# Two gathers in one product, sums evacuated bank by bank: a graph attention layer with gathered neighbours

## The chip, the cores and the metric

The kernel runs on one core of a Trainium2 chip. The metric is the device time of one execution in microseconds. The time before is the median of three runs. A hardware profile comes from one further execution.

## The reference

Two layers work on 4096 nodes of 128 features and a random 4096 x 4096 adjacency of density 1/128, so that a node has some 32 neighbours.

Layer 0 is graph attention with eight heads. For a head with weights `W`, node n weighs its neighbours m:

```
Wh  = nodes @ W                       # per head
e   = leaky_relu(f1[n] + f2[m], 0.2)  # f1 = Wh . a1, f2 = Wh . a2
att = softmax(where(adj > 0, e, -9e15))
h   = elu(att @ Wh)                   # heads side by side: 1024 features
x   = layernorm(nodes + elu(h @ W1 + b1))
```

Layer 1 takes, for each node and feature, three quantiles over the values of its neighbours (some neighbours left out by a rule), mixes their mean with the node's own value, and applies one 128 x 128 matrix.

## The kernel before

**Stages.** A search on DVE and PE turns each adjacency row into a list of at most 64 neighbours. Nodes are then ranked by their count, and 128 nodes of similar count form a tile; `CAPS` gives for each tile the number of neighbour slots it must hold. There are 32 tiles in three blocks of 2, 8 and 22 (`BLOCKS`). While the tiles of block 0 and 1 are weighed, the search for the next block runs between them; the tiles of block 2 have no search beside them. When all are done, layer 1 (`quantile_out`) gathers values again and runs a selection network on DVE.

**Attention of one tile.** The sum over neighbours is taken on the raw node rows, and `W` is applied afterwards. `layers(cap)` cuts the slots into layers of 32, 16, 8 or 4. `fetch_rows` loads the tile's records (SP queue), transposes indices and f1 scores (DVE) and issues one indirect gather per slot column on POOL's queue (line 185), 128 rows each of 137 words: 128 features, a one, eight f2 scores. In a layer of w slots, one gathered column g holds all w slots of k = 128 / w nodes. The rows go into the buffers `G` (32 columns; two of them, and in block 2 a third in another pool) or `Gs` (16 columns, two).

`weigh_rows` then does, per layer: `z` = exp(leaky_relu(f2 + f1)) (DVE lines 829 and 830, ScalarE line 831); `pf`, the weights spread over the columns of the nodes that own them (DVE line 835, 1024 elements a partition); and one product per gathered column (PE line 847), `pf` piece by rows, with 129 columns: weighted features and, from the one, the denominator. Its output goes to `y`, three PSUM banks that hold eight blocks of 129 columns; a block is 16 nodes times 8 heads on 128 partitions. A 32-slot layer gives 32 products into 32 partitions each, a 16-slot layer 16 into 64, a small layer 8 into 128. The products of one layer are finished before those of the next layer.

When all layers are summed, DVE takes the denominators out of PSUM (`rden`, lines 868 and 875) and writes the normalised sums `yn` to SBUF (line 879). PE transposes `yn` in two halves (`turned`, line 896), ScalarE copies them to `yT` (line 897). For two or four tiles together, `transform` applies `W`, elu, `W1`, elu and the layer norm, and the rows go out by scatters on POOL's queue (line 194, `x_d`).

**Order.** `step` fetches tile i and then weighs tile i-1, so POOL gathers one tile ahead. `weigh_rows` is a generator; after each of its yields ("turns") `step` runs one turn of a waiting `transform` and a share of the search pieces:

```
turns = sum(2 + -(-w // 8) for w, *_ in parts) + 3
each = -(-quota // turns)
```

With `quota` 48 pieces a tile in block 0 and 33 in block 1. In these two blocks the order on DVE, PE and ScalarE is as written (`manual_schedule`); in block 2 a scheduler orders the instructions. `pp` holds the PSUM tiles `y` (three banks), `turned`, `o` and `hT`; `key` of the search has the last two banks.

Of the kernel before, what the change touches and what calls it, by code (L numbers as in the profile page):

```python
# [9 lines left out]
F32 = mybir.dt.float32  # L10
# [3 lines left out]
ALU = mybir.AluOpType  # L14
# [6 lines left out]
P = 128  # L21
N = 4096
D = 128
H = 8
# [4 lines left out]
TINY = 1e-30  # L29
# [33 lines left out]
LMAX = 2 * max(HT)  # L63
LMOST = 2 * sorted(HT)[-2]
TURN = 12


R_NUM, R_OWN, R_F1 = L, L + 1, L + 2
# [6 lines left out]
def layers(c):  # L75


    out = []
    s = 0
    for w in (32, 32, 16, 8, 4):  # L80
        if (c + 3) // 4 * 4 - s >= w:
            out.append((s, w))
            s += w
    return out
# [124 lines left out]
def kernel(  # L209
# [135 lines left out]
    def step(fetch=None, pieces=None, quota=0, size=2, more=None):  # L345
        if fetch:
            weigh.append(fetch_rows(tc, pools, narrow[turn[0] % 2], *fetch, xt_d, bad, uses))
            turn[0] += 1
        while store:
            scatter(nc, x1_d, *store.pop(0))  # L350
        if len(weigh) > 1 or (weigh and not fetch):
            R, parts = weigh.pop(0)
            place = len(members)
            members.append(R)
            turns = sum(2 + -(-w // 8) for w, *_ in parts) + 3
            each = -(-quota // turns)
            done = 0
            for _ in weigh_rows(tc, attp, pools, pp, parts, turned, place, size, consts):
                if tails and next(tails[0], True):
                    tails.pop(0)  # L360
                for _ in range(min(each, quota - done)):
                    next(pieces, None)
                    done += 1
            quota -= done
            if len(members) == size:
                tails.append(
                    transform(tc, attp, pp, more or pp, turned.pop(0), list(members), consts, store)
                )
                members.clear()
        elif not fetch:  # L370
            while tails:
                if next(tails[0], True):
                    tails.pop(0)
        for _ in range(quota):
            next(pieces, None)
# [379 lines left out]
def fetch_rows(tc, ap, narrow, rec_d, i, cap, t, xt_d, bad, turn):  # L755

    nc = tc.nc

    R = take(ap, [P, REC], "R", turn, 5)
    rows = rec_d[ts(i, P), :]  # L760
    for u, v in enumerate(rows.rearrange("(g u) w -> u g w", u=4)[k] for k in range(4)):
        nc.sync.dma_start(R[ts(u, 32), :], v)
    for s0, w in layers(cap):
        if w == 32:
            continue
        r = 32 // w
        lists, scores = narrow[w]
        v = rows.rearrange("(g b r) w -> b g r w", b=4, r=r)
        for b in range(4):
            here = slice(32 * b, 32 * b + w)  # L770
            nc.sync.dma_start(
                lists[here, :].rearrange("p (r j) -> p r j", r=r),
                v[b].bitcast(I32)[:, :, s0 : s0 + w],
            )
            nc.sync.dma_start(scores[here], v[b][:, :, R_F1 : R_F1 + H])
    nc.vector.tensor_scalar(
        bad[:, 4, t : t + 1], R[:, R_NUM : R_NUM + 1], float(cap), None, ALU.is_gt
    )
    f1x32 = None
    parts = []  # L780
    G, col = None, 0
    for s0, w in layers(cap):
        k = P // w
        idx = ap[0].tile([P, 32], I32, name="idx", bufs=6)
        if w == 32:
            nc.vector.transpose(idx, R.bitcast(I32)[:, s0 : s0 + w])
            scores, r = R[:, R_F1 : R_F1 + H].unsqueeze(1), 1
        else:
            lists, scores = narrow[w]
            r = 32 // w  # L790
            nc.vector.transpose(idx, lists)
        if w < 32 or f1x32 is None:
            f1b = ap[0].tile([P, H, 32], F32, name="f1b", bufs=1)
            nc.vector.tensor_copy(
                f1b.rearrange("p h (r j) -> p r h j", r=r),
                scores.unsqueeze(3).to_broadcast([P, r, H, 32 // r]),
            )
            f1x = ap[0].tile([P, 32 * H], F32, name="f1x", bufs=6)
            nc.vector.transpose(f1x, f1b.rearrange("p h g -> p (h g)"))
        if w == 32:  # L800
            f1x32 = f1x
        f1v = f1x.rearrange("p (h g) -> p g h", h=H)[:, 0:w, :]
        if w == 32:
            G, col = take(ap, [P, 32, XW], "G", turn), 0
        elif s0 % 32 == 0:

            few = sum(v for s, v in layers(cap) if s >= s0) <= 16
            G, col = take(ap, [P, 16 if few else 32, XW], "Gs" if few else "G", turn), 0
        for g in range(w):
            gather(nc, G[:, col + g, :], xt_d, idx[:, g : g + 1])  # L810
        parts.append((w, k, G[:, col : col + w, :], f1v))
        col += w
    return R, parts


def weigh_rows(tc, ap, pools, pp, parts, turned, place, size, consts):


    nc = tc.nc
    own, ident = consts["own"], consts["ident"]  # L820

    y = pp.tile([P, 3, 512], F32, name="y")

    def block(b):
        return y[:, b // 3, (b % 3) * (D + 1) : (b % 3 + 1) * (D + 1)]

    for i, (w, k, G, f1v) in enumerate(parts):
        z = ap.tile([P, 32, H], F32, name="z")[:, 0:w, :]
        nc.vector.tensor_tensor(z, G[:, :, D + 1 :], f1v, ALU.add)
        nc.vector.scalar_tensor_tensor(z, z, ALPHA, z, ALU.mult, ALU.max)  # L830
        nc.scalar.activation(z, z, AF.Exp)  # L831
        yield
        pf = ap.tile([P, H * P], F32, name="pf")
        spread = [P, w, k, H]
        nc.vector.tensor_tensor(
            pf.rearrange("p (g k h) -> p g k h", g=w, k=k),
            z.unsqueeze(2).to_broadcast(spread),
            own[w].unsqueeze(1).unsqueeze(3).to_broadcast(spread),
            ALU.mult,
        )  # L840
        yield
        last = i == len(parts) - 1
        m = min(k * H, P)
        for g in range(w):
            for c in range(g * k * H, (g + 1) * k * H, m):
                b, p0 = c // P, c % P
                nc.tensor.matmul(  # L847
                    block(b)[p0 : p0 + m, :],
                    lhsT=pf[:, c : c + m],
                    rhs=G[:, g, 0 : D + 1],  # L850
                    start=(i == 0 and b % 3 == 0),
                    stop=last,
                    skip_group_check=True,
                )
            if g % 8 == 7 or g == w - 1:
                yield

    rden = ap.tile([P, H], F32, name="rden")
    yn = ap.tile([P, H, P], F32, name="yn", bufs=1)
    spans = ((0, 2, 6), (2, 1, 2))  # L860
    views = []
    for bank, banks, n in spans:
        c = n // banks
        views.append(
            y[:, bank : bank + banks, 0 : c * (D + 1)].rearrange("p a (c d) -> p a c d", c=c)
        )
    for (bank, banks, n), v in zip(spans, views):
        nc.vector.tensor_scalar(  # L868
            rden[:, 3 * bank : 3 * bank + n].rearrange("p (a c) -> p a c", a=banks),
            v[:, :, :, D],  # L870
            TINY,
            None,
            ALU.max,
        )
    nc.vector.reciprocal(rden, rden)
    for (bank, banks, n), v in zip(spans, views):
        here = slice(3 * bank, 3 * bank + n)
        c = n // banks
        nc.vector.tensor_tensor(
            yn[:, here, :].rearrange("p (a c) d -> p a c d", a=banks),  # L880
            v[:, :, :, 0:D],
            rden[:, here]
            .rearrange("p (a c) -> p a c", a=banks)
            .unsqueeze(3)
            .to_broadcast([P, banks, c, D]),
            ALU.mult,
        )
    yield
    if place == 0:
        wide = [P, H, size * P]  # L890
        turned.append(pools[0 if size == 2 else -1].tile(wide, F32, name="yT" if size == 2 else "yT4", bufs=1))
    yT = turned[-1]
    for half in range(2):
        t_ps = pp.tile([P, 4, P], F32, name="turned")
        for b in range(4):
            nc.tensor.transpose(t_ps[:, b, :], yn[:, 4 * half + b, :], ident)  # L896
        nc.scalar.copy(  # L897
            yT[:, :, ts(place, P)].rearrange("p h (u g) -> p g u h", u=4)[:, ts(half, 16)],
            t_ps.rearrange("p b (g u h) -> p (b g) u h", u=4, h=H),
        )  # L900
        yield
# [493 lines left out]
```

## Time and profile before

| | us |
|---|---|
| runs | 4465.6, 4467.9, 4470.0 (median 4467.9) |
| profiled execution | 4423.5 |
| its span, first to last instruction | 4421.7 |

| engine | busy us | share of the span |
|---|---|---|
| PE matmul | 975.6 | 22% |
| PE weight load | 518.4 | 12% |
| DVE | 2531.5 | 57% |
| ScalarE (ACT) | 1028.7 | 23% |
| POOL | 2301.1 | 52% |

How to read the profile: a group's row names line, engine, operation, output and input tile, the count, the busy time with the mean duration in ns, and the idle time of the engine just before these instructions with what ended it. "issue" as the end of a wait means that nothing in the trace released the engine. A row of waits gives who waited for whom, then the total in us, the number of waits and the longest. A row of the timeline gives start, duration, engine, line, operation, names, count, and in brackets the idle time before it. A row of windows gives a stretch, its length, busy time and number of instructions of PE, PE's weight loads, DVE, ScalarE and POOL, the granted share of PE's clock, the busy share of the DMA engines, and GB/s. An fp32 product of PE stands in the trace as two records, each with a weight load; a transpose as one.

### The profile page before, as it was taken

How to read it: one execution, taken by the hardware profiler on the slowest of the kernel's cores; microseconds unless marked ns; L12 is line 12 of the kernel's file. 1: busy time of each engine (PE TensorE's matmuls, PEld its weight loads, DVE VectorE, ACT ScalarE, POOL GpSimd, SP SyncE). 2: the span in 40 equal slices, each digit the busy share in tenths (PEclk: the TensorE clock that was granted, in tenths of full speed). 3: DMA queues.
4: the chain of work that ended last, by engine and by line, in shares of the span. 5: the costliest groups of instructions: out<-in, count | busy, mean ns of one | idle time of the engine just before them, and what ended most of it. 6: DMA issues, size and time to landing. Idle time of an engine off the chain costs nothing. (4 is left out here: it accounts for less than half of the span.)

```text
span 4421.7 us, 19775 instructions
## 1 busy us (share of the span) xinstructions
PE 975.6 (22%) x4289; PEld 518.4 (12%) x4289; DVE 2531.5 (57%) x4862; ACT 1028.7 (23%) x1424; POOL 2301.1 (52%) x2453
## 2 busy tenths in 40 slices
PE   4323544443223133223243000000000001000101
PEld 2001211111112011121122000000000000000001
DVE  5554556555322114112121437888878999999897
ACT  2101212111000011000010213333333444434343
POOL 2433443344667666757564675666575334455530
PEclk9955555556556555555565555555555555555555
DMA  5313323221121121212111111111111001111100
GB/s 169 108 47 113 99 90 111 86 92 42 48 50 50 47 56 44 57 42 56 44 49 32 48 52 39 48 46 47 35 49 37 23 21 33 31 36 36 38 28 3
DMA packets 115233, 241.26 MB, mean 55 GB/s; under 512 B 51904, under 2 KB 68288, under 8 KB 106912
## 3 DMA queue, kind: packets, MB, share of 16 engines
q0 software_dynamic: 76224, 161.01, 13.2%
q10 hardware_dynamic: 12160, 68.49, 4.4%
q1 hardware_dynamic: 26720, 10.41, 1.1%
q14 instruction: 93, 0.76, 0.1%
q8 instruction: 36, 0.59, 0.1%
HBM read 228.56 MB, written 11.18 MB: 54 GB/s over the span
## 5 line engine op out<-in xcount | busy, mean ns | idle before, releaser
L1145 DVE TENSOR_TENSOR vals<-low,vals 128x1024 f32<-128x1024 f32 (+9 forms) x1359 | 1401.9, 1057 | 332.5 <-ACT low L1141 110.6
L185 POOL DMA_INDIRECT G<-xt_d,idx x1092 | 1066.0, 976 | 729.1 <-issue 399.3
L185 POOL DMA_INDIRECT vals<-x_d,idx x960 | 910.6, 948 | 296.0 <-issue 282.3
L1141 ACT COPY low<-vals 128x1024 f32<-128x1024 f32 (+10 forms) x701 | 607.2, 876 | 969.7 <-DVE vals L1145 658.1
L1155 PE MATMUL st_ps<-ident,u 128*128 128x128 f32 x344 | 86.9, 436 | 1773.9 <-ACT u L1154 1445.8
L577 DVE MAX8 first<-key 128x8 f32<-128x128 f32 x1024 | 223.5, 282 | 342.5 <-remote 207.6
L194 POOL DMA_INDIRECT out_dram<-o,own_i x32 | 31.8, 992 | 619.0 <-ACT o L1167 616.5
L847 PE MATMUL y<-G,pf 128*32 128x129 f32 (+2 forms) x2224 | 211.5, 398 | 525.7 <-issue 428.9
L1155 PEld LDWEIGHTS st_ps<-ident,u 128*128 128x128 f32 x344 | 75.5, 325 | 1785.0 <-ACT u L1154 1453.5
L571 PE MATMUL key<-sgn,markb 128*128 128x512 bf16 x256 | 147.8, 577 | 529.2 <-DVE first L577 358.3
L868 DVE TENSOR_SCALAR rden<-y 128x6 f32<-128x6 f32 x64 | 7.3, 152 | 398.9 <-PE y L847 217.8
L847 PEld LDWEIGHTS y<-G,pf 128*32 128x32 f32 (+2 forms) x2224 | 141.9, 171 | 599.5 <-issue 483.0
L550 ACT ACTIVATE sgn<-adj_t 128x2048 bf16<-128x2048 int32 x64 | 122.0, 1906 | 355.8 <-PE key L571 177.1
L897 ACT COPY yT<-turned 128x512 f32<-128x512 f32 x64 | 65.5, 1024 | 554.8 <-PE turned L896 356.0
L917 DVE TENSOR_SCALAR e<-e 128x512 f32<-128x512 f32 x64 | 28.4, 444 | 241.0 <-issue 203.8
L573 PE MATMUL key<-parts,oneb 64*128 64x512 bf16 x256 | 146.5, 572 | 1.1 <-issue 1.0
L925 PE MATMUL o<-hv,W_sb 128*128 128x256 f32 (+1 forms) x176 | 105.3, 717 | 143.8 <-DVE hv L919 53.5
L194 POOL DMA_INDIRECT x_d<-x,R x32 | 33.4, 1044 | 194.6 <-DVE x L986 161.8
L1145 DVE TENSOR_TENSOR most<-low,most 128x1024 f32<-128x1024 f32 (+7 forms) x116 | 131.8, 1166 | 2.6 <-issue 0.5
L185 POOL DMA_INDIRECT Gs<-xt_d,idx x92 | 89.7, 975 | 77.8 <-PE y L847 46.1
L584 DVE MAX8 rec<-first 128x8 f32<-128x256 f32 x256 | 109.2, 426 | 30.8 <-remote 16.9
L831 ACT ACTIVATE z<-z 128x256 f32<-128x256 f32 (+3 forms) x62 | 20.3, 329 | 452.0 <-DVE z L830 351.6
(187 smaller groups left out, 1795.9 us busy)
## 6 DMA issues: line engine op xcount, KB each, us to landing
adj_t<-in_adj_dram ACTq DMA_DIRECT2D x64, 1024.0 KB
G<-xt_d,idx POOLq DMA_INDIRECT x1092
vals<-x_d,idx POOLq DMA_INDIRECT x960
R<-rec_d SPq DMA_DIRECT2D x128, 26.4 KB
xt_d<-rec SPq DMA_DIRECT2D x4, 548.0 KB
score<-rec_d SPq DMA_DIRECT2D x132, 1.0 KB
rec<-in_x_dram SPq DMA_DIRECT2D x4, 512.0 KB
Gs<-xt_d,idx POOLq DMA_INDIRECT x92
```

Source lines behind the costliest of these rows:

```text
L185: nc.gpsimd.indirect_dma_start(out=dst, out_offset=None, in_=rows, in_offset=bass.IndirectOffsetOnAxis(ap=idx, axis=0),)
L550: nc.scalar.activation(sgn, adj_t, AF.Sign, accum_out=cnt[:, i : i + 1])
L571: nc.tensor.matmul(key, lhsT=markb, rhs=sgn[:, ts(b, 512)], start=True, stop=False)
L573: nc.tensor.matmul(key, lhsT=oneb[0:64, :], rhs=parts[:, c0 : c0 + 512], start=False, stop=True)
L577: nc.vector.max(first[:, ts(c0 // CW + c, 8)], key[:, ts(c, CW)])
L584: nc.vector.max(top, first)
L847: nc.tensor.matmul(block(b)[p0 : p0 + m, :], lhsT=pf[:, c : c + m], rhs=G[:, g, 0 : D + 1], start=(i == 0 and b % 3 == 0), stop=last, skip ...
L897: nc.scalar.copy(yT[:, :, ts(place, P)].rearrange("p h (u g) -> p g u h", u=4)[:, ts(half, 16)], t_ps.rearrange("p b (g u h) -> p (b g) u ...
L925: nc.tensor.matmul(o, lhsT=consts["W1_sb"][:, h, :], rhs=hv[:, ts(j, n)], start=(h == 0), stop=(h == H - 1),)
L1141: nc.scalar.copy(kept, low)
L1145: nc.vector.tensor_tensor(high if end else low, kept, high, ALU.max if end else ALU.min)
L1155: nc.tensor.matmul(st_ps, lhsT=u, rhs=ident, start=(i == 0), stop=(i == len(terms) - 1))
```

## The change

All layers' `z` are computed first. Then the tile is worked through in two halves of four blocks. For each half, `pf` is written for every layer (512 elements a partition). For each block there is one PSUM bank, `y`, out of three in turn. In a 32-slot layer (and in a 16-slot layer where that is the widest), the `pf` pieces of two gathered columns are loaded together, and both columns' rows are streamed side by side: 258 columns. Of the four parts of the product, the two where weights and rows belong to the same gathered column are wanted. The other layers stream their one column twice, so that both halves of the bank receive it. ScalarE then copies the wanted halves, 32 or 64 partitions at a time, to `raw` in SBUF, and DVE normalises `raw` in place.

The turns counted for the search pieces change with the new yields, and `Gs` has 12 columns.

```diff
+YBANKS = 3
...
-            turns = sum(2 + -(-w // 8) for w, *_ in parts) + 3
+            turns = len(parts) + 13
...
-            few = sum(v for s, v in layers(cap) if s >= s0) <= 16
-            G, col = take(ap, [P, 16 if few else 32, XW], "Gs" if few else "G", turn), 0
+            few = sum(v for s, v in layers(cap) if s >= s0) <= 12
+            G, col = take(ap, [P, 12 if few else 32, XW], "Gs" if few else "G", turn), 0
...
-    y = pp.tile([P, 3, 512], F32, name="y")
...
+    zs = []
+    for w, k, G, f1v in parts:
+        z = ap.tile([P, 32, H], F32, name="z", bufs=4)[:, 0:w, :]
         nc.vector.tensor_tensor(z, G[:, :, D + 1 :], f1v, ALU.add)
         nc.vector.scalar_tensor_tensor(z, z, ALPHA, z, ALU.mult, ALU.max)
         nc.scalar.activation(z, z, AF.Exp)
+        zs.append(z)
         yield
...
+    split = 2 if parts[0][0] == 32 else 1
+    raw = ap.tile([P, H, D + 1], F32, name="raw", bufs=1)
+    for half in range(2):
+        pfs = []
+        for (w, k, G, _), z in zip(parts, zs):
+            g2 = w // 2
+            pf = ap.tile([P, H * P // 2], F32, name="pf", bufs=5)
...
+            pfs.append(pf)
         yield
...
+        for b in range(4):
+            y = pp.tile([P, 512], F32, name="y", bufs=YBANKS)[:, 0 : 2 * (D + 1)]
+            yv = y.rearrange("p (a d) -> p a d", a=2)
+            for i, ((w, k, G, _), pf) in enumerate(zip(parts, pfs)):
+                both = w == 32 or (w == 16 and split == 1)
+                m = max(min(k * H, P) * (2 if both else 1), 32)
+                for p0 in range(0, P, m):
+                    c = b * P + p0
+                    g = half * (w // 2) + c // (k * H)
+                    if both:
+                        rhs = G[:, g : g + 2, 0 : D + 1]
+                    else:
+                        rhs = G[:, g : g + 1, 0 : D + 1].to_broadcast([P, 2, D + 1])
+                    nc.tensor.matmul(
+                        yv[p0 : p0 + m],
+                        lhsT=pf[:, c : c + m],
+                        rhs=rhs,
+                        start=(i == 0),
+                        stop=(i == len(parts) - 1),
+                        skip_group_check=True,
+                    )
+            m = P // (2 * split)
+            for p0 in range(0, P, m):
+                a = p0 // m % 2
+                nc.scalar.copy(raw[p0 : p0 + m, 4 * half + b, :], yv[p0 : p0 + m, a, :])
+            yield

     rden = ap.tile([P, H], F32, name="rden")
-    yn = ap.tile([P, H, P], F32, name="yn", bufs=1)
...
+    nc.vector.tensor_scalar(rden, raw[:, :, D], TINY, None, ALU.max)
     nc.vector.reciprocal(rden, rden)
...
+    yn = raw[:, :, 0:D]
+    nc.vector.tensor_tensor(yn, yn, rden.unsqueeze(2).to_broadcast([P, H, D]), ALU.mult)
     yield
```

More of the change, by code (lines that the diff above doesn't have):

```diff
@@ L820, in weigh_rows @@
     own, ident = consts["own"], consts["ident"]
-    y = pp.tile([P, 3, 512], F32, name="y")
[L824 to L828, printed above, removed]
+    zs = []
+    for w, k, G, f1v in parts:
+        z = ap.tile([P, 32, H], F32, name="z", bufs=4)[:, 0:w, :]
         nc.vector.tensor_tensor(z, G[:, :, D + 1 :], f1v, ALU.add)
@@ L831, in weigh_rows @@
         nc.scalar.activation(z, z, AF.Exp)
+        zs.append(z)
         yield
[L833 to L840, printed above, removed]
-        yield
[L842 to L856, printed above, removed]
@@ L858, in weigh_rows @@
-    rden = ap.tile([P, H], F32, name="rden")
-    yn = ap.tile([P, H, P], F32, name="yn", bufs=1)
[L860 to L887, printed above, removed]
+    split = 2 if parts[0][0] == 32 else 1
@@ new lines, in weigh_rows @@
+    raw = ap.tile([P, H, D + 1], F32, name="raw", bufs=1)
[4 more added lines that the diff above has]
+            pf = ap.tile([P, H * P // 2], F32, name="pf", bufs=5)
+            spread = [P, g2, k, H]
+            nc.vector.tensor_tensor(
+                pf.rearrange("p (g k h) -> p g k h", g=g2, k=k),
+                z[:, ts(half, g2), :].unsqueeze(2).to_broadcast(spread),
+                own[w].unsqueeze(1).unsqueeze(3).to_broadcast(spread),
+                ALU.mult,
+            )
+            pfs.append(pf)
+        yield
+        for b in range(4):
[18 more added lines that the diff above has]
+                        skip_group_check=True,
+                    )
+            m = P // (2 * split)
[3 more added lines that the diff above has]
+            yield
```

## The prediction

> **What bounds the kernel now.** I first cut the span at the two places where POOL's work changes: the first gather of the third block (1178 us) and the first gather of the second layer (2444 us). Busy time of each engine in these three stretches:
>
> ```profile
> core 0: us, PE busy (x) PEld busy (x) DVE busy (x) ACT busy (x) POOL busy (x), PEclk, DMA share, GB/s
> 0.00:1178.00 1178.00, 453.33 (x1727) 182.60 (x1727) 629.15 (x2350) 191.44 (x270) 466.55 (x552) 0.63 0.30 93
> 1178.00:2444.00 1266.00, 375.09 (x2026) 215.98 (x2026) 263.62 (x690) 105.91 (x157) 802.80 (x816) 0.57 0.19 48
> 2444.00:4422.00 1978.00, 147.19 (x536) 119.78 (x536) 1638.70 (x1823) 731.36 (x997) 1031.70 (x1086) 0.51 0.12 36
> ```
>
> The last stretch is the quantile network, DVE's, and the change touches nothing in it. The first holds ten node tiles between pieces of the neighbour search, in written order on DVE, PE and ScalarE. The middle one holds 22 tiles and is paced by POOL: 776 gathers of about 0.98 us and 0.30 us to the next, some 990 of 1266 us. What POOL waited for there:
>
> ```profile
> POOL G L185 <- issue: 211.3, 693, 0.3
> POOL G L185 <- PE y L847: 51.6, 2, 36.3
> POOL x_d L194 <- DVE x L986: 47.3, 2, 26.0
> POOL Gs L185 <- PE y L847: 46.1, 3, 21.9
> ...
> POOL G L185 <- PE turned L896: 7.0, 1, 7.0
> POOL G L185 <- DVE rden L875: 5.9, 1, 5.9
> ```
>
> The first row is 0.3 us a gather. The rows on y, turned and rden are gather buffers that a late attention tile has not given back: 110.6 us, the part within the change's reach. The x_d row is the end, where the second layer waits for the last tiles. Why is PE late with only 375 us busy? PE's own waits and its timeline say it:
>
> ```profile
> PE y L847 <- issue: 438.6, 175, 65.3
> ```
> ```profile
> 1554.51 3.67 PE L847 MATMUL y<-G,pf 128*32 128x129 f32 x64 [4.09 <-DVE pf L835]
> ```
> ```profile
> 1819.16 1.48 PEld L847 LDWEIGHTS y<-G,pf 128*32 128x32 f32 x31 [4.97 <-DVE pf L835]
> 1819.16 1.94 PE L847 MATMUL y<-G,pf 128*32 128x129 f32 x30 [3.40 <-DVE pf L835]
> ...
> 1821.80 0.37 PE L847 MATMUL y<-G,pf 128*32 128x129 f32 x1 [0.69 <-issue]
> 1822.50 0.12 PEld L847 LDWEIGHTS y<-G,pf 128*32 128x32 f32 x1 [1.86 <-issue]
> 1823.90 0.38 PE L847 MATMUL y<-G,pf 128*32 128x129 f32 x1 [1.73 <-issue]
> 1825.30 0.13 PEld L847 LDWEIGHTS y<-G,pf 128*32 128x32 f32 x1 [2.67 <-issue]
> ```
>
> A matmul in fp32 is two records, each with its weight load. The same 64 records of a 32-slot layer took 3.67 us at 1554, while no gather ran; at 1819 some 31 pairs went at once, and the other 33 took until 1911: 2.7 us a pair, starts in multiples of 0.70 us, each ended by "issue". Such stretches come only while gathers run at their full pace with DVE idle, and end 5 to 15 us after the last gather. The first of these two windows is one, the second is not:
>
> ```profile
> 1822.00:1916.00 94.00, 14.25 (x38) 5.65 (x38) 0.00 (x0) 0.00 (x0) 59.86 (x64) 0.50 0.19 48
> 1706.00:1770.00 64.00, 22.13 (x238) 16.08 (x237) 46.56 (x118) 11.01 (x14) 47.93 (x41) 0.60 0.19 48
> ```
>
> In the middle stretch I count eight of them, 358 us in all (1516, 1666, 1822, 1941, 2099, 2179, 2289, 2301). So PE is late by its **number of instructions**, not by its arithmetic.
>
> [...] 64 records in 3.67 us are 52 ns each against 226 ns for 128-column ones (16 in 3.81 us at 762)[...].
>
> **The change part by part.**
> *Matmuls.* The layers in the kernel are 29 of 32 slots, 6 of 16 and 27 of 8 or 4 (records 1856, 192 and 432 at 64, 32 and 16 a layer). Now 32 slots take 16 matmuls for 32, 16 slots take 8 for 16 (all six are in tiles without a 32-slot layer), the small ones stay at 8. Matmuls: 29x16 + 6x8 + 27x8 = 728 for 1240; with four instructions each, 2048 PE instructions fewer, 64 for a usual tile of 160.
> *Stream.* Each streams 258 columns for 129[...]. From 52, 106 and 226 ns a record: 29x3.3 + 6x3.4 + 27x3.6 = 213 us before, 29x6.8 + 6x7.2 + 27x7.2 = 435 us after: +222 us of PE, 6.9 us a tile[...].
> *Evacuation.* 26 tiles x 32 + 6 x 16 = 928 new ScalarE copies of 129 elements. Nearest rows: 128-wide copies out of PSUM, 263 ns (L1160) and 267 ns (L510)[...]. At 265 ns: 246 us, 8.5 us a usual tile[...]. 32 partitions instead of 128 I take to save nothing. Behind them in ScalarE's queue stand the next exp, yT and, in the first stretch, the sign of the next adjacency half; PE waits for a copy before it reuses one of three banks. A bank costs PE 1.7 us and ScalarE 1.1 us, so ScalarE follows.
> *DVE.* pf in halves: 124 of about 0.68 us (hv, 128x512, 0.69) for 62 of 1.22: +9 us. Two rden and two yn (7.3 + 43.6 us) become one each, at 0.15 and about 1.2 us (pf's 1024 elements): -8. Together nil, under POOL or search work; without that cover 0.3 us a tile.
> *Order.* No matmul starts before every layer's exp and pf; G comes free only with the last bank. Before, the first layer could run while a second was still being gathered. That costs at most a small layer's gathers, 5 to 10 us, and nothing where the next tile's gathers are already running, as here. raw has one buffer, as yn had. Turns per tile go from 12 to 15, so the search pieces end four turns before the tile does: in the first stretch DVE may wait 3 to 4 us a tile for the last bank and its copies. The 16-slot small buffer becomes 12; no cap leaves 13 to 16 slots, so no tile moves. No DMA is added or moved: SP, POOL and DMA queues keep their instructions and order.
>
> *Sum, middle stretch.* A tile in a 0.70 us stretch: 160 instructions[...], seen as 94 us from 1822 to 1916. [...] I keep 40% of the 110.6 us, for tiles with three layers, for transposes and transforms (not cut), and for two late tiles in a row: **-66 us**. Bounds: 0 and -110.
> *End.* The tile before the last held PE until 2394, 15 us after the last gather (2379). That goes; the last tile has two 32-slot layers, +7 us of stream and +1 us of copies: **-7 us**, between -15 and +10.
> *First stretch.* The ten tiles pay 6.9 us of PE and 8.5 us of ScalarE each where PE is 38% busy and ScalarE 16%, and gain 64 instructions of some 330 a tile where DVE waited 207.6 us for PE's results at the same creeping pace (19 waits, the longest 31.4 us). A fifth of 208 is -42; a 4 us tail on ten tiles is +40. I take **0**, between -60 and +90.
>
> Sum: 66 + 7 = 73; 4423.5 - 73 = 4350 us for the profiled execution (span 4421.7). It lies 44 us under the median of the runs, 4467.9; I move the difference over unchanged: **4395 us**.
>
> **The rivals.**
> *A, slower: the copies and the longer stream lie open in the first stretch.* Its order is fixed, so a copy that waits for PE holds the sign behind it, and a matmul that waits for its bank holds the key matmul that DVE needs. If 9 of the 15.4 us a tile show: +90; with the creeping stretches eased by only 40 us in the middle, +50: 4518 us. It decides from about 7 us a tile in the first stretch. For it: each tile there now needs eight hand-overs between PE and ScalarE, where the creep delays PE's. Against: ScalarE has 84% idle, three banks give slack, and DVE, the fullest, gets no work.
> *B, hidden anyway.* POOL's waits shift rather than go: the late buffer is followed by late lists (DVE f1b, 34.5 us in the middle) or by a search wait. Half of the -73, with 20 us lost in front: -15, 4453 us. Against: four of the large gaps end right where a creeping stretch does (1706, 1919, 2157, 2214).
> *C, it does not do what it says:* column-paired matmuls pay by column in the creeping stretches, not by instruction. Then 64 half-count instructions of double length take as long as now and the stream is added: +20 us, 4488. Against: the starts step by 0.70 us though a record's busy time is 0.37 us.
>
> **How the numbers follow.** Forecast 0.62, A 0.18, B 0.15, C 0.05. The likeliest gives 4395, by its bounds 4290 to 4470. For 8 in 10 the range goes up to A's nearer half, 4500, and down to 4295. 0.2% is 9 us, about what a measurement of this kernel can tell from no change. Forecast faster in nearly all its range, B in about two thirds: faster 0.72, same 0.05, slower 0.23.
>
> **What would show it.** Right: y matmuls at 1456 records, 258 columns; PE's "issue" wait before y under half of 438.6 us; POOL's waits for y, turned and rden at 20 to 60 us; the second layer's first gather some 70 us before 2444; ScalarE up by about 200 to 250 us. Wrong: the first gather of the third block later than 1178 by 40 us or more (A); POOL's waits on f1b or the copies grown by what y lost (B); y records starting at twice the spacing in creeping stretches (C).

## The result: slower by 0.8%, where a gain of 1.6% was forecast

The changed kernel took 4503.4 us (median of four runs, 4497.6 to 4506.7) beside 4466.8 us of the kernel before: ratio 1.0078, 95% interval 1.0064 to 1.0091. Timed again in the second set of runs it gave 1.0092 (1.0070 to 1.0113). Its profiled execution took 4500.2 us.

One thing has to be known to read the numbers. In the first comparison and in the sets one and two the kernel before took 4431 to 4467 us, and PE crept behind the gathers as the prediction describes: while gathers ran, its records started 0.70 us or a multiple of it apart. In all later sets it took 3827 to 3833 us, with the same instructions at the same durations (search MAX8 285 ns in before_again and 283 ns in before_tailfast, gather 973 and 975 ns), and PE's records no longer stood in steps of 0.70 us: its waits before y that nothing in the trace ends came to 438.8 us in the middle stretch of before_again, and in that of before_d they are not among the seven largest of its waits, the last of which is 1.4 us. I call the two "with creep" and "without creep"; the time of every kernel is compared only with the kernel before of its own set. The profiled execution of before in the prediction (4423.5 us) was 43 us shorter than its runs, so stages are compared through a second profile of before, from the set that also ran the changed kernel (`before_again`, `after_again`).

The windows of the changed kernel, cut as in the prediction at the first gather of the third block and of the second layer (columns as there):

```profile
core 0: us, PE busy (x) PEld busy (x) DVE busy (x) ACT busy (x) POOL busy (x), PEclk, DMA share, GB/s
0.00:1204.00 1204.00, 513.01 (x1352) 189.87 (x1361) 634.54 (x2360) 273.47 (x577) 473.57 (x553) 0.66 0.31 91
1204.00:2514.00 1310.00, 444.89 (x1368) 215.90 (x1368) 263.25 (x678) 262.62 (x778) 789.23 (x815) 0.61 0.20 46
2514.00:4499.00 1985.00, 147.24 (x536) 119.87 (x536) 1639.83 (x1823) 731.33 (x997) 1034.80 (x1086) 0.50 0.13 36
```

The middle stretch has a third fewer PE records (1368 for 2026) and is longer, 1310 for 1266 us. DVE and POOL do what they did, ScalarE has its copies. What POOL waited for there (waiter, line, releaser: us in all, times, longest):

```profile
POOL x_d L195 <- DVE x L978: 94.5, 4, 32.0
POOL G L186 <- PE y L861: 65.1, 4, 17.4
POOL Gs L186 <- PE y L861: 52.4, 3, 22.8
...
POOL Gs L186 <- remote: 13.7, 2, 6.9
```

The waits for late attention tiles, which the change was forecast to cut, are all there: 117.5 us on y against 97.7. In `after_again` they are 90.9 us against 100.5 in `before_again`. New is part of the first row: scatters of finished rows that wait for x, 94.5 us against 47.3. Two of its four waits, 37.6 us, stand in the middle of the stretch with gathers behind them in the queue; the other 56.8 us are at its end, where those of before are. PE's wait in front of y that nothing in the trace ends was to fall under half of 438.6 us; it is

```profile
PE y L861 <- issue: 406.8, 37, 62.5
```

and its timeline shows the form that the creep has taken:

```profile
1554.41 1.20 PE L861 MATMUL y<-G,pf 128*64 128x258 f32 x4 [7.65 <-issue]
1562.82 1.20 PE L861 MATMUL y<-G,pf 128*64 128x258 f32 x4 [7.21 <-issue]
1572.70 1.20 PE L861 MATMUL y<-G,pf 128*64 128x258 f32 x4 [8.68 <-issue]
1583.96 1.20 PE L861 MATMUL y<-G,pf 128*64 128x258 f32 x4 [10.06 <-issue]
1595.19 1.20 PE L861 MATMUL y<-G,pf 128*64 128x258 f32 x4 [10.03 <-issue]
```

Each row is one bank of a tile: four records in 1.20 us. Then PE stands until the next bank. The starts are 8.4, 9.9, 11.3 and 11.2 us apart; the last two are 16 steps of 0.70 us.

Stages on the timeline, in us (ends of the first and middle stretch are the first gather of the third block and of the second layer):

| kernel | first ends | middle | last | span |
|---|---|---|---|---|
| with creep: before_again | 1195.4 | 1271.9 | 1982.7 | 4450.0 |
| with creep: after_again | 1206.2 | 1298.6 | 1982.1 | 4486.9 |
| without creep: before_d | 912.4 | 1087.2 | 1825.5 | 3825.1 |
| without creep: after_c | 986.7 | 1082.1 | 1825.0 | 3893.8 |

With creep the loss is 10.8 us in the first stretch and 26.7 in the middle, and these two are not sharp. The first stretch of before_again ends 17 us later than in the first profile of before. The middle stretch has the same instructions in before, before_again and before_early (a run below), and took 1265.8, 1271.9 and 1279.6 us; in after, after_again and spread (below) it took 1309.7, 1298.6 and 1280.9. Without creep the loss is larger (after_c: ratio 1.0171), and all of it, 74 us, lies in the first stretch. Without creep, the kernels that were profiled twice agree within 6 us in each stage.

### The profile page after: what moved, and what is told of

It reads as the page before. It is cut to its first block, busy times and chain, and to the rows that moved or that the text cites. A ratio compares the mean times of both kernels' runs of the same rounds, so it can differ in the third digit from the quotient of the medians.

```text
span 4498.4 us, 19115 instructions
## 1 busy us (share of the span) xinstructions
PE 1105.1 (25%) x3256; PEld 525.6 (12%) x3265; DVE 2537.6 (56%) x4860; ACT 1267.4 (28%) x2352; POOL 2297.6 (51%) x2453
## 5 line engine op out<-in xcount | busy, mean ns | idle before, releaser
L872 ACT COPY raw<-y 32x129 f32<-32x129 f32 (+1 forms) x928 | 240.0, 259 | 980.2 <-remote 548.8
L861 PE MATMUL y<-G,pf 128*64 128x258 f32 (+1 forms) x1200 | 310.7, 548 | 538.4 <-issue 383.2
L861 PEld LDWEIGHTS y<-G,pf 128*64 128x64 f32 (+1 forms) x1200 | 142.5, 199 | 680.3 <-issue 495.4
L840 DVE TENSOR_TENSOR pf<-z,own 128x512 f32<-128x512 f32 x124 | 80.8, 683 | 169.1 <-remote 50.4
L917 PE MATMUL o<-hv,W_sb 128*128 128x256 f32 (+1 forms) x176 | 94.1, 650 | 153.2 <-DVE hv L911 87.2
```

What stands on the lines that cost most here:

```text
L840: nc.vector.tensor_tensor(pf.rearrange("p (g k h) -> p g k h", g=g2, k=k), z[:, ts(half, g2), :].unsqueeze(2).to_broadcast(spread), own[w] ...
L861: nc.tensor.matmul(yv[p0 : p0 + m], lhsT=pf[:, c : c + m], rhs=rhs, start=(i == 0), stop=(i == len(parts) - 1), skip_group_check=True,)
L872: nc.scalar.copy(raw[p0 : p0 + m, 4 * half + b, :], yv[p0 : p0 + m, a, :])
L917: nc.tensor.matmul(o, lhsT=consts["W1_sb"][:, h, :], rhs=hv[:, ts(j, n)], start=(h == 0), stop=(h == H - 1),)
```

## The experiments

The expectations name theories by letters. H: the hand-overs bank by bank between PE and ScalarE. S: the longer stream of the paired products. C: the 928 small copies (in the prediction, C is another rival). Q: the search pieces that now end four turns before a tile does. A: the prediction's rival. E: PE's completions that reach ScalarE late while gathers run. X: the place of the scatters in POOL's queue.

### Set one, with creep (before 4431.6 us)

The expectations in microseconds were set against 4467 us for the kernel before. It took 4431.6 here, so they are read as ratios to it.

**nohand**: three banks used in turn without being read between blocks, all copies after the last product. Five of the eight sums of a tile are lost.

```diff
+    ys = [pp.tile([P, 512], F32, name=f"y{i}", bufs=1)[:, 0 : 2 * (D + 1)] for i in range(3)]
...
-            y = pp.tile([P, 512], F32, name="y", bufs=YBANKS)[:, 0 : 2 * (D + 1)]
-            yv = y.rearrange("p (a d) -> p a d", a=2)
+            yv = ys[(4 * half + b) % 3].rearrange("p (a d) -> p a d", a=2)
...
-                nc.scalar.copy(raw[p0 : p0 + m, 4 * half + b, :], yv[p0 : p0 + m, a, :])
             yield
...
+    for b in range(H):
+        yv = ys[b % 3].rearrange("p (a d) -> p a d", a=2)
+        for p0 in range(0, P, m):
+            a = p0 // m % 2
+            nc.scalar.copy(raw[p0 : p0 + m, b, :], yv[p0 : p0 + m, a, :])
```

> The changed kernel with the copies of all eight blocks after the last product of the tile; blocks 3 to 7 overwrite the three banks unread, so five of eight sums are lost. Products, their 258 columns, and the 928 copies stay. Theory H (each of the eight hand-overs from PE to ScalarE inside a tile pays PE's late completions while gathers run): the hand-overs go, the halved instruction count stays, so below the kernel before: 4400 us (4360 to 4455), the middle stretch (first gather of block 3 to first gather of layer 1) at or under 1260 us. Theory S (the doubled stream): still 4500. Theory Q (the search pieces end early in the first stretch): 4480 to 4500, with the middle stretch as in the changed kernel, 1310 us.

Measured: 4494.9 us, ratio 1.0135 (1.0118 to 1.0152), middle 1308.2 us. Without a hand-over between blocks the tile is no faster. The time has moved to the end of the tile: PE's wait before the transposes that nothing ends is 338.1 us. One tile in a creeping stretch, PE and then ScalarE:

```profile
1561.34 4.37 PE L861 MATMUL y<-G,pf 128*64 128x258 f32 x30
1649.40 1.09 PE L890 MATMUL turned<-ident,raw 128*128 128x128 f32 x4 [83.70 <-issue]
```
```profile
1606.01 0.79 ACT L875 COPY raw<-y 32x129 f32<-32x129 f32 x3 [43.52 <-remote]
1617.16 1.07 ACT L875 COPY raw<-y 32x129 f32<-32x129 f32 x4 [10.37 <-remote]
1628.37 3.71 ACT L875 COPY raw<-y 32x129 f32<-32x129 f32 x14 [10.14 <-issue]
1633.24 0.26 ACT L875 COPY raw<-y 32x129 f32<-32x129 f32 x1 [1.16 <-issue]
1634.63 0.26 ACT L875 COPY raw<-y 32x129 f32<-32x129 f32 x1 [1.13 <-issue]
```

PE's products start at once, in 4.37 us. ScalarE starts to copy 44.7 us after the first of them and goes on at 11.2 us, the pace of the changed kernel's banks; its last copies start 1.40 us apart, two steps of 0.70. From the first product to the last copy it is 86 us. So H in its plain form falls: what is paid is the way from PE's products to the end of ScalarE's copies, wherever it stands.

**unpaired**: the eight banks stay, but each gathered column has its own product of 129 columns, and a bank is one copy of 128x129.

```diff
-                m = max(min(k * H, P) * (2 if both else 1), 32)
+                m = min(k * H, P)
...
-                        rhs=rhs,
+                        rhs=G[:, g, 0 : D + 1],
...
-                nc.scalar.copy(raw[p0 : p0 + m, 4 * half + b, :], yv[p0 : p0 + m, a, :])
+            nc.scalar.copy(raw[:, 4 * half + b, :], yv)
```

> The changed kernel with one product of 129 columns per gathered column, as before, still block by block through three banks; one copy of 128 partitions per bank, 8 a tile instead of 32. H: the eight hand-overs are there and the instruction count is that of before, so as slow as the changed kernel or slower, 4500 to 4560. S: the stream is that of before, so the loss goes: 4460 to 4475. Theory C (the 928 small copies on ScalarE): 8 for 32 copies, so most of the loss goes: about 4475.

Measured: 4483.3 us, 1.0107 (1.0089 to 1.0125), middle 1316.7 us. Without the paired stream the ratio is no better than the changed kernel's 1.008 to 1.009, so on balance the stream is not what costs; with it went the saving in records (2024 in the middle stretch). What a record costs in a creeping stretch can be read from this run:

```profile
1573.76 0.66 PE L855 MATMUL y<-G,pf 128*32 128x129 f32 x8 [17.84 <-issue]
1596.11 0.66 PE L855 MATMUL y<-G,pf 128*32 128x129 f32 x8 [21.68 <-issue]
1618.50 0.66 PE L855 MATMUL y<-G,pf 128*32 128x129 f32 x8 [21.74 <-issue]
```

A bank of eight records of 129 columns stands 22.4 us, 32 steps of 0.70. The changed kernel's bank of four records of 258 columns stood 11.2 us, 16 steps. Both are 2.8 us a record, whatever its width.

**before_act**: the kernel before, but ScalarE copies its three banks and DVE normalises in SBUF.

```diff
+    for bank, n in ((0, 3), (1, 3), (2, 2)):
+        nc.scalar.copy(
+            raw[:, 3 * bank : 3 * bank + n, :].rearrange("p c d -> p (c d)"),
+            y[:, bank, 0 : n * (D + 1)],
+        )
...
+    nc.vector.tensor_tensor(yn, yn, rden.unsqueeze(2).to_broadcast([P, H, D]), ALU.mult)
```

> The kernel before with only the evacuation changed: three ScalarE copies of whole banks after the tile's last product, DVE normalises in SBUF. H: one hand-over as before, so 4460 to 4480, no change that can be told. C[...]: 4485 or more.

Measured: 4454.4 us, 1.0050 (1.0033 to 1.0067); the first stretch ends at 1177.3 us and the middle is 1290.9, beside 1265.8 to 1279.6 in the three profiles of before's middle. DVE's multiplication itself is not slower in SBUF (39.1 us in all for 43.6; 39.3 in the profile of the changed kernel). Putting ScalarE between PE and DVE costs 0.5% on its own, with three copies a tile; H had no change for it. By the profiles it is the stretch where PE creeps behind the gathers.

**spread**: the changed kernel with its search pieces shared out evenly over all turns.

```diff
-            each = -(-quota // turns)
...
-                for _ in range(min(each, quota - done)):
+                at += 1
+                for _ in range(min(-(-quota * at // turns), quota) - done):
```

> The changed kernel with the search pieces spread evenly over all turns instead of the same number at each until they are used up. Q: the first stretch loses its 25 us, 4475. H: the hand-overs stay, and pieces later in the tile only cover them in part: 4490 to 4500, the middle stretch unchanged at 1300 to 1320.

Measured: 4423.9 us, 0.9983 (0.9972 to 0.9994); first stretch to 1164.2 us. This one edit takes back the whole loss. Its middle stretch, 1280.9 us, is shorter too, though the edit moves nothing there and H had 1300 to 1320 for it; that part is not explained.

### Set two, with creep (before 4454.4 us)

**after_again** and **before_again** are the two kernels as they are.

> The changed kernel as it is, timed again beside the kernel before on the chip that also runs the next kernels, so that stages are compared within one chip. Every theory: ratio 1.007 to 1.010. Theory Q (search pieces end four turns before the tile's end): its first stretch ends about 40 us after that of the kernel with spread pieces (1164.2 there, 1204.0 here).

> The kernel before as it is, for a profile on this chip. If the chips differ, its stages move against the first profile (first stretch to 1178.5, middle 1265.8, last 1977.4 us); if only runs differ, they stay within 10 us.

Measured: after_again 4491.6 us, 1.0092 (1.0070 to 1.0113); before_again 4451.9 us; stages in the table above. Stages of single profiles differ by some 17 us with creep, so the 42 us between the first stretches of after_again and spread rest on the ratios as well (1.0092 and 0.9983).

**before_early**: the kernel before, pieces ending four turns early (`turns - 4` in spread's formula).

> The kernel before, with nothing changed but that the search pieces of a tile end four turns earlier (so the last products, the normalising and the two transposes have no search piece beside them). Theory Q, that the uncovered end of a tile costs the changed kernel its loss: first stretch 20 to 40 us longer than before, the middle the same, time 4450 to 4475 where before is 4431. Theory A of the prediction (hand-overs through ScalarE in the first stretch): no more than 8 us, since there are none here.

Measured: 4447.9 us, 0.9992 (0.9981 to 1.0004), first stretch to 1170.7. So Q as a general rule falls. In the kernel before an early end costs nothing.

What differs is seen in DVE's waits of the first stretch. Before z it waits 24.1 us in before_again, 61.9 in after_again (53.0 of it for gathers), 42.9 in spread; in before_early no such row is left. Before bad (line 777), for a tile's records, it waits 61.9, 79.8, 54.6 and 54.3 us in this order. The waits sit at the borders of the blocks. The changed kernel has the z of all layers ahead of the first product, and the next tile's z has nothing before it on DVE once the pieces are used up; in the kernel before the first layer's products ran while the second layer was being gathered (tile 2: first product at 456 us in before_again, at 495 in after_again).

**onecopy_spread**: spread, with one copy of 128x129 per bank, which leaves half of the rows with the other column's sums.

> The changed kernel with evenly spread search pieces and one copy of 128x129 per bank in place of four (or two) copies of 32 (64) rows: 256 copies where there were 832; half the rows then take the wrong gather's sums, so the output is left wrong and only the time is read. If ScalarE's chain of four copies per bank is what the products wait for in the middle stretch: about 0.8 us less per bank, 8 banks and some 10 tiles per stretch there, 15 to 30 us less than the spread kernel (4424). If the wait is for the products' own late completion, which one copy must await as well: within 5 us of it in the middle stretch.

Measured: 4427.2 us, 0.9950 (0.9931 to 0.9968), middle 1277.8 us against spread's 1280.9. Nearly three in four copies less (256 for 928) bring 0.3% in the ratio, some 15 us, which is the lower edge of what was put on ScalarE's row of copies. The middle differs by 3 us, but from a profile of another set, which is not sharp enough to place the 15 us. So the row of copies costs a little; whether in the middle stretch stays open.

### Sets three to six, without creep (before 3828.6 to 3833.0 us)

In after_again POOL waits 90.3 us for x in the middle stretch, in before_again 47.5. `step` advances a waiting `transform` once per turn; with 14 to 16 turns a tile for 9 to 15 it ends a tile earlier, and its scatters stand ahead of gathers 228, 608, 880 and 1036 in POOL's queue and no more ahead of 264, 640, 916 and 1076. Two kernels exchange this: **tailpace** is the changed kernel with the old number of advances, **before_tailfast** the kernel before with the new number. The order of scatters and gathers in POOL's queue is in before_tailfast exactly that of the changed kernel. In tailpace it is that of the kernel before but for two scatters, which stand ahead of gather 408 where before has them ahead of 516 and 520. **tailpace_spread** adds the even pieces, **unpaired_tps** to these also the single products of `unpaired`.

```diff
+            paced = sum(2 + -(-w // 8) for w, *_ in parts) + 3
...
-                if tails and next(tails[0], True):
-                    tails.pop(0)
+                if tails and stepped < paced:
+                    stepped += 1
+                    if next(tails[0], True):
+                        tails.pop(0)
```

> The changed kernel, but a tile's turns advance the transform of earlier tiles only as many times as in the kernel before (9 to 13 times per tile in place of 14 to 16), so that the scatters of x1 stand again on POOL's queue behind gathers 264, 640, 916 and 1076, where the changed kernel had moved them ahead of these (228, 608, 880 and 1036). Theory X, that the loss is the gathers standing behind scatters whose x is not ready (POOL's waits for x in the middle stretch 90.3 us in the changed kernel, 47.5 before): the waits fall back to about 48, the middle stretch from 1299 to about 1260 to 1275, ratio 0.998 to 1.002. Theory E, late completions of the bank products: the order of POOL's queue does not matter, ratio 1.007 to 1.010.

> The kernel before, with one thing changed: the transform of earlier tiles is advanced 14 to 16 times per tile, spread over the 9 to 13 turns, as often as in the changed kernel; POOL's queue then has the scatters exactly where the changed kernel has them. Products, copies, banks and search pieces are those of before. Theory X: 25 to 40 us slower, ratio 1.006 to 1.009, the middle stretch 1295 to 1310. Theory E, or any theory in which products, hand-overs or copies carry the loss: within 0.2% of before.

> The same with the search pieces spread evenly over the turns. Theory X plus the measured effect of spreading (-1.1% in total on the changed kernel, nearly all in the first stretch): ratio 0.988 to 0.993, that is faster than both. Theory E: as the kernel with spread pieces alone, 0.998.

> The kernel of tailpace_spread with single products of 129 columns and one copy of 128x129 per bank in place of paired products of 258 and four copies of 32 rows. Tells what pairing is worth once the queue order and the pieces are put right. If the pairing pays in the middle stretch (fewer products where PE creeps behind the gathers): 10 to 20 us slower than tailpace_spread. If the middle is set by the gathers and scatters alone: within 5 us of it.

Measured in set three: tailpace 1.0200 (1.0186 to 1.0214), before_tailfast 0.9924 (0.9910 to 0.9937), tailpace_spread 1.0054 (1.0040 to 1.0068), unpaired_tps 1.0007 (0.9999 to 1.0016). All expectations of size missed, because the waits that they are about did not arise without creep. They were run again:

> The kernel of tailpace again, for a chip in the condition of the original measurement (the kernel before near 4450 us, PE's records 0.70 us and multiples apart behind gathers), since the third set of runs met one without such steps (before 3833 us). Near 4450: theory X (gathers queued behind scatters that wait for x) ratio 0.998 to 1.002, the middle stretch 1260 to 1275 us; theory E (late completions) 1.007 to 1.010. Near 3830: as there, 1.02, since no wait for x over 25 us was left in the middle stretch to be taken away.

> The kernel of before_tailfast again, for the same reason. Near 4450: theory X 1.006 to 1.009 with POOL's waits for x in the middle stretch going from 48 to about 90 us; theory E within 0.2% of before. Near 3830: 0.992 as in the third set.

> The kernel of tailpace_spread again, for the same reason. Near 4450: theory X 0.988 to 0.993, theory E 0.998. Near 3830: 1.005.

> The changed kernel as it is. Near 4450: 1.007 to 1.010 as twice before. Near 3830: between tailpace (1.020) and 1.0; theory E (its loss comes from PE completions that creep behind gathers) says that the middle stretch is then no longer than that of the kernel before with its scatters moved (1080), and that what is left of the loss is the first stretch.

Measured: 1.0208 (1.0195 to 1.0221), 0.9932 (0.9919 to 0.9945), 1.0057 (1.0044 to 1.0070), and after_c, the changed kernel itself, 3894.2 us, 1.0171 (1.0156 to 1.0185). Again no creep. What E said of after_c held: its middle stretch is 1082.1 us where 1080 was put, and the loss is in the first stretch. What these say without creep is plain: an earlier transform is a gain, 0.7% in the kernel before and 0.4% in the changed one (tailpace against after_c). X is wrong there, and was never tried with creep. before_tailfast, the kernel before with nothing but this changed, is as fast against its kernel before as the best of the changed kernels (unpaired_spread below, 0.9940).

> The kernel before as it is, for its profile in the condition of this chip. Near 3830: if the loss of the changed kernel there (65 us) is in the first stretch alone, the middle stretch here is 1078 to 1084 us as in all the kernels of the third and fourth sets, and the first stretch ends at 915 to 925 (986.7 in the changed kernel), with DVE as busy in it as there (584 us) and its waits some 65 us shorter. Near 4450: as before_again, middle stretch near 1270.

before_d took 3826.8 us and settles where the loss lies without creep. Waits and windows of DVE in the first stretch, first of before_d:

```profile
96.00:912.00 816.00, 390.79 (x1585) 151.64 (x1591) 580.04 (x2154) 165.30 (x192) 451.47 (x463) 0.62 0.36 114
```
```profile
DVE first L577 <- PE key L573: 91.6, 131, 9.8
DVE bad L776 <- DMA R<-rec_d: 61.6, 2, 36.2
DVE z L829 <- DMA G<-xt_d,idx: 31.4, 2, 29.1
```

then of after_c:

```profile
96.00:987.00 891.00, 452.81 (x1225) 161.19 (x1225) 584.42 (x2164) 247.59 (x499) 454.34 (x465) 0.64 0.34 105
```
```profile
DVE first L578 <- PE key L574: 123.3, 143, 9.7
DVE bad L777 <- DMA R<-rec_d: 78.1, 2, 46.1
DVE z L826 <- DMA G<-xt_d,idx: 55.3, 4, 19.1
...
DVE rden L876 <- ACT raw L872: 9.3, 3, 3.7
```

DVE is busy for 580 and 584 us; its idle time (length less busy) goes from 236 to 307 us, +71, and that is the loss. Most of it stands in the rows: search pieces that wait for their key products +31.7, z for gathers +23.9, records +16.5, normalising for the copies +9.3, less 18.4 that the kernel before had in front of pf, a row that is gone. The timeline of after_c shows a piece behind a bank:

```profile
607.57 1.13 PE L861 MATMUL y<-G,pf 128*64 128x258 f32 x4
...
608.62 1.23 PE L861 MATMUL y<-Gs,pf 128*128 128x258 f32 x2
...
609.64 0.63 PE L572 MATMUL key<-sgn,markb 128*128 128x512 bf16 x1
...
610.85 0.89 DVE L578 MAX8 first<-key 128x8 f32<-128x128 f32 x4 [2.29 <-PE key L574]
```

The bank holds PE for 2.3 us, half of it for the small layer, whose one column is streamed twice. The next key product comes after it, and DVE, which had caught up, stands 2.29 us. PE is busy for 453 us in this stretch where it was for 391.

**unpaired_spread**: even pieces, single products, one copy per bank, the transform's new pace.

> The changed kernel with evenly spread search pieces, single products of 129 columns and one copy per bank, and the transform advanced once per turn as in the changed kernel. If the effects add up: near 3830, unpaired_tps (1.0007) less what the transform's own pace is worth (after_c 1.0171 against tailpace_b 1.0208, -0.4%), 0.995 to 0.999; near 4450, unpaired (1.0107) less what spreading is worth (spread 0.9983 against the changed kernel 1.008 to 1.009, -1.0%), 0.998 to 1.003. If the pieces only mattered because pairing delays the bank's end, spreading brings less here: 1.003 or more.

Measured: 3808.5 us, 0.9940 (0.9927 to 0.9954), faster than both kernels and just past the 0.995 to 0.999 that the sum of the effects gave; with creep it was not run. Its DVE waits (window 96 to 906, DVE busy 583.4 us):

```profile
DVE first L578 <- PE key L574: 83.6, 127, 10.0
DVE bad L777 <- DMA R<-rec_d: 66.9, 2, 35.0
DVE z L826 <- DMA G<-xt_d,idx: 36.7, 4, 22.6
```

The wait for key products is below that of before_d, and the idle time is down to 227 us. tailpace_spread and unpaired_tps differ by the pairing alone, with its copies: 1.0054 and 1.0007, so without creep pairing costs 0.5%. The rest of the difference is where the pieces stand: tailpace to tailpace_spread is 1.5%.

## Why the prediction was wrong

**Counts and durations held.** y products 1456 records of 258 columns; ScalarE 1267.4 for 1028.7 us, +239 where 246 was worked out (258 ns a copy of 32 partitions; the prediction took 265, after 263 and 267 for 128 partitions); DVE 2537.6 for 2531.5. PE's stream was taken too high: busy +130 us, not +222.

**The step that failed is the middle stretch's sum for a creeping tile.** Forecast -66 us with bounds 0 and -110; the time from the third block's first gather to the last one grew by 20 (1204.9 to 1224.6, before_again and after_again). The sum lets the first instructions of a tile go free, and only the rest creep. How many go free was the author's estimate; in the prediction's trace 61 went at once at 1819 (31 weight loads and 30 products). By the sum a tile with one 32-slot layer, now 32 records or 64 instructions, would hardly creep at all, and its gather buffer would be back in time. In the profile of the changed kernel such a tile takes 85 us from its first product at 1543.84 to the end of its last copy at 1628.73, nearly as long as the 94 us creep that was to go: 12 records, three banks, start at once, in 2.92 us, and from there on the banks of four start 8.4 to 11.3 us apart. Over the tile that is 2.7 us for each of the 32 records, and no longer only for those behind the first, which in the prediction's window were 33 of 64. So the halved count of records did its work, and the free start was lost with it. Taking the waits between banks away does not bring it back: nohand has none inside a tile, the 30 records that its trace has of a tile start in 4.4 us, and its tile takes 86 us all the same. A start of PE is early; what ScalarE waits for is late (44.7 us after the first product in nohand). Why, no run shows. "A bank costs PE 1.7 us and ScalarE 1.1 us, so ScalarE follows" has the same gap: it counts the work of a hand-over and not its way. Smaller than this: the row of the prediction's 94 us window has 38 records, 76 instructions, where 61 gone at once would leave 99 of a tile's 160.

**A term was left out.** "No DMA is added or moved" is wrong in its order: the turns that were counted for search pieces also advance the transform, and the scatters moved up in POOL's queue. With creep POOL's wait for x rose by 43 us (47.5 to 90.3, before_again and after_again), of which 33.9 us stand ahead of gathers. How much of the 27 us in the middle is this and how much the hand-overs stays open. The swap was run only without creep, and there an earlier transform helps. Two things speak for the creep's part: without creep the middle stretch is 5 us shorter, not 27 longer; and before_act, whose scatters did not move, lost its 0.5% in the middle too.

**The end** was forecast at -7 and came at +7 (last gather to the second layer's first 67.0 to 74.0 us). Without creep it came at +6 (38.8 to 45.0), so it fits the +8 that the prediction gave to the last tile's longer products and copies; the saving on the tile before it did not come.

**The first stretch** was taken as 0, between -60 and +90, and came at +11 with creep. Both halves of that sum exist: waits before the search's first fell by 63 us (340 to 278, all releasers together) where -42 was put, and the waits at the end of tiles rose by 18 (records) and 38 (z) where +40 was put. But the second was described as a tail on every tile; it is at the borders of the blocks. Without creep the first half has nothing to save and turns into a loss of 32, so the sum is +74: nearly rival A's size (+90). A's mechanism, a key product behind a bank, is seen in the timeline of after_c; the 32 us are what this wait grew by in all. Its sign was set at 40 us; with creep 11 to 25 was seen.

**Rival B** is right about the middle stretch where PE does not creep: there POOL's own gathers set it (no wait for y is among the seven largest of POOL in either kernel's middle stretch), and 658 records of PE fewer change 5 us. With creep its sign, waits on f1b that grow, did not show (34.9 us before, 23.8 after). **Rival C** falls: records of 129 and of 258 columns take the same 2.8 us in creeping stretches (unpaired and the changed kernel).

## What to carry to other kernels

Where a change splits work into pieces that two engines hand to each other, price the hand-over by the delay that the trace shows between a product and the other engine's start in that stage. An engine's early start is worth something only if the engine behind it gets the result early too: in nohand a tile's products ran in 4.37 us, and the copies ended 86 us after the first of them. When the number of turns changes, look for everything that is driven once per turn: here the search pieces and, by way of the transform, the scatters in another engine's queue; setting the pieces right brought 1.0% with creep and 1.5% without. And before pricing a gain on a pace that no instruction accounts for, ask what the kernel looks like without it.

## What the runs showed of the hardware

The same kernel took 4450 us and 3827 us at equal instruction durations. What differed were steps of 0.70 us between an engine's instructions while gathers run. They were seen on PE and on ScalarE. On PE a product record took four steps: 2.8 us each in the prediction's window, 11.2 us for a bank of four, 22.4 us for a bank of eight in unpaired. On ScalarE single copies of 0.26 us started 1.40 us apart in nohand. The quantile stretch, which the change leaves alone, also differs (1982 and 1825 us). What brings this pace about no run shows. The record has the same chip number, 6, for set one, with creep, and set three, without, so the chip alone does not explain it.
